# Gather buffers cut from seven to three in an edge-message kernel

## Chip, cores and metric

The kernel runs on one core of one Trainium2 chip. The metric is the device time of one execution in microseconds; lower is better.

## What is computed

A graph layer with N = 6250 nodes of H = 128 features and E = 100000 edges, sorted by target `dst`, each with 4 edge features:

```python
msg_in = jnp.concatenate([node_features[src], node_features[dst], edge_features], axis=1)
h = jax.nn.silu(msg_in @ mW1 + mb1)
messages = h @ mW2 + mb2
aggregated = jax.ops.segment_sum(messages, dst, num_segments=N)
upd_in = jnp.concatenate([node_features, aggregated], axis=1)
u = jax.nn.silu(upd_in @ uW1 + ub1)
updated = u @ uW2 + ub2
return layer_norm(node_features + updated, ln_g, ln_b)
```

The result is added to x and normalized once more. All in float32.

## The kernel before

**Tables.** The product with `mW1` is split by its rows. For all nodes the kernel computes `tab_a = x @ mW1[:128]` and `tab_b = x @ mW1[128:256] + mb1` and stores both in HBM: a loop of 13 blocks for tab_a (L196 to L199), then one for tab_b (L209 product, L211 addition on VectorE into one of three `tb` tiles, L212 store by SyncE's queue). Every edge then needs a row of tab_a by its source, a row of tab_b by its target, and its own 4 features.

**Lists.** Edge features are transposed (L242) and stored (L243), the indices of all groups but the first 14 are loaded (L248, L249), and the targets are made relative to a base node per group (L250). The queue of SyncE in this prologue is in the order written.

**Edges.** Edges go in 98 groups of 1024, eight of 128 each. For a group g:

- `fetch(g)` takes a tile `ga` of 128 x 8 x 128 floats from the pool `gath` and fills it with eight indirect DMAs issued by GpSimd (POOL), one row of tab_a for each edge (L281). In this stage nothing else is on POOL's queue, so POOL runs ahead of the loop as far as free tiles of the pool allow.
- `load(g)` has SyncE load the window of 96 rows of tab_b, the edge features and the targets (L328 to L334); `matrices(g)` makes one-hot matrices of the targets on VectorE (L341, L349).
- `hidden(g)`: TensorE sums the window rows and edge features of each edge (`pre`, L361), VectorE adds the gathered rows (`s = ga + pre`, L363), ScalarE applies silu (L365). The addition L363 is the last reader of `ga`: after it, the tile is free.
- `by_nodes` (L372, L374) sums the messages of one group by node on TensorE, and `add` (L379 to L383) adds the transposed sums into `acc`.

The loop over g issues, in program order, the fetch of a later group, the loads of g+2, the matrices of g+1, `hidden(g)`, `by_nodes(g-1)` and `add(g-2)`. The tile framework puts in the waits, so a gather into a tile waits for the addition L363 of the group that held this tile before.

**Update.** When all groups are summed, the nodes go through the second pair of products and two normalizations (L404 to L499). A second, general path (L502) runs only for lists whose targets don't fit the windows.

Of the kernel before, what the change touches and what calls it, by code (L numbers as in the profile page):

```python
# [24 lines left out]
def kernel(  # L25
# [49 lines left out]
    NW = NP + W  # L75
    K1 = W + ED
    RB = 14
    AHEAD = 4
    LEAD = 2
    FIRST = 14  # L80
    XC = 8
# [101 lines left out]
    with tc.tile_pool(name="tables", bufs=3) as work, tc.tile_pool(  # L183
        name="tables_ps", bufs=2, space=PSUM
# [53 lines left out]
    with tc.tile_pool(name="lists", bufs=1) as work, tc.tile_pool(  # L238
        name="lists_ps", bufs=1, space=PSUM
# [48 lines left out]

    with ExitStack() as edges:
        held = edges.enter_context(tc.tile_pool(name="held", bufs=1))  # L290
        gath = edges.enter_context(tc.tile_pool(name="gath", bufs=AHEAD + 3))
        work = edges.enter_context(tc.tile_pool(name="edge", bufs=3))
        ps = edges.enter_context(tc.tile_pool(name="edge_ps", bufs=2, space=PSUM))

# [11 lines left out]
        def fetch(g):  # L306
            if g >= NG:
                return
            rows[g] = gath.tile([P, G, H], F32, name="ga")
            for i in range(G):  # L310
                gather(rows[g][:, i, :], tab_a, src_i[:, g, i : i + 1])
# [12 lines left out]
        def load(g):  # L324

            if g % RB == 0:
                load_bases(g)
            nc.sync.dma_start(mv[g % NM][:W], tab_b[bass.ds(bases[g], W), :])  # L328
            nc.sync.dma_start(stbuf[g % NST][W:], ea_d[:, g * GE : (g + 1) * GE])
            near[g] = work.tile([W, GE], I32, name="near")  # L330
            n = min(GE, E - g * GE)
            if n < GE:
                nc.vector.memset(near[g][:, n:], N)
            nc.sync.dma_start(  # L334
                near[g][:, :n],
                dst[g * GE : g * GE + n].rearrange("(o e) -> o e", o=1).to_broadcast([W, n]),
            )
# [47 lines left out]
        for g in range(LEAD):  # L385
            load(g)
        for g in range(AHEAD):
            fetch(g)
        oh, h, sw = {0: matrices(0)}, {}, {}
        for g in range(NG + 2):  # L390
            fetch(g + AHEAD)
            if g + LEAD < NG:
# [250 lines left out]
```

## Time and profile before

| | |
|---|---|
| median of 3 runs | 1214.57 us (1214.18 to 1215.01) |
| profiled execution | 1460.16 us, of it the span 1458.3 us |
| mean granted TensorE clock in it | 0.681 |
| busy share of the span: PE, PEld, DVE, ACT, POOL | 56%, 50%, 27%, 14%, 58% |
| gathers (L281) | 784, 1017 ns each |
| DMA | 114.63 MB, mean 79 GB/s |

The profiled execution is 245.6 us longer than the median, far more than the difference between runs, so shares of it can't be carried over to the timed runs without a check. "PE" is TensorE's matmuls, "PEld" its weight loads, DVE VectorE, ACT ScalarE, POOL GpSimd, SP SyncE; a q behind an engine's name means its queue. L281 is line 281. A group's line reads: line, engine, operation, tiles, count, then total busy time, mean ns of one, then the idle time before them and what ended most of it.

### The profile page before, as it was taken

The page shows a single profiled execution, that of the slowest core. Times are in us where ns is not written, and L with a number is a line of the kernel's source. Part 1 is how long each engine was busy: PE and PEld are TensorE (multiplying, and loading weights), DVE is VectorE, ACT ScalarE, POOL GpSimd, SP SyncE. Part 2 cuts the span into 40 slices and gives each one's busy share as a digit, 9 for nine tenths or more (in the row PEclk, how much of TensorE's full clock was granted, in tenths as well). Part 3 has the DMA queues.
Part 4 walks back from the last instruction along what each step waited for, and adds up shares of the span by engine and source line. Part 5 has one row for each costly group of instructions (what it writes and reads, how often), then busy time and mean ns, then how long its engine had stood idle before and what let it go on. Part 6 is the DMA issues. An engine that isn't in the chain of part 4 may idle for free.

```text
span 1458.3 us, 11699 instructions
## 1 busy us (share of the span) xinstructions
PE 816.6 (56%) x3782; PEld 727.7 (50%) x3782; DVE 400.1 (27%) x803; ACT 197.9 (14%) x340; POOL 838.8 (58%) x814
## 2 busy tenths in 40 slices
PE   5410565837564673765726726756576647699700
PEld 5300455727453572655716726745465636594300
DVE  2101331313221231222303303323122212344543
ACT  1002110101110110111101101101011101112254
POOL 3670267657666766766667667666766666604110
PEclk9655566757656775667757757757665666689955
DMA  8424532323232332322323323322322222300011
GB/s 203 121 67 88 103 84 79 100 67 98 83 86 67 87 100 58 95 80 82 91 58 96 89 60 96 89 68 84 87 76 80 82 72 82 90 5 0 2 50 39
DMA packets 100906, 114.63 MB, mean 79 GB/s; under 512 B 42245, under 2 KB 78094, under 8 KB 100758
## 3 DMA queue, kind: packets, MB, share of 16 engines
q1 hardware_dynamic: 72358, 60.68, 14.8%
q0 software_dynamic: 25088, 51.43, 13.8%
q10 hardware_dynamic: 3392, 1.70, 0.5%
q8 instruction: 32, 0.52, 0.1%
q14 instruction: 36, 0.29, 0.1%
HBM read 102.47 MB, written 11.28 MB: 78 GB/s over the span
## 4 chain that ended last, share of the span: by engine, by line
PE 48%; issue 26%; another core or an unknown queue 14%; DVE 4%; ACT 4%; SPq 2%; DMA 1%; POOL 1%; DVEq 0%; ACTq 0%
PE pre L361 23%; PE pw L372 17%; ACT o L490 1%; ACT z L475 1%; SPq L128 1%; PE pa L196 1%; PE ps_y L437 1%; PE ps_a L423 1%; DVE s L363 1%; PE ps_u L427 1%; PE pt L380 1%; DVE st L416 1%; PE ps_u L428 1%; PE ps_a L422 1%
## 5 line engine op out<-in xcount | busy, mean ns | idle before, releaser
L281 POOL DMA_INDIRECT ga<-tab_a,src_i x784 | 797.1, 1017 | 464.9 <-issue 227.4
L361 PE MATMUL pre<-mv,st 100*128 100x128 f32 x1568 | 417.6, 415 | 145.2 <-issue 139.1
L361 PEld LDWEIGHTS pre<-mv,st 100*128 100x128 f32 x1568 | 392.5, 333 | 158.4 <-issue 157.3
L372 PE MATMUL pw<-h,oh 128*96 128x129 f32 x1568 | 301.2, 339 | 271.3 <-issue 266.2
L372 PEld LDWEIGHTS pw<-h,oh 128*96 128x96 f32 x1568 | 258.3, 213 | 310.4 <-issue 305.5
L363 DVE TENSOR_TENSOR s<-ga,pre 128x1024 f32<-128x1024 f32 x98 | 119.3, 1217 | 387.9 <-remote 222.1
L349 DVE TENSOR_TENSOR oh<-w_row,rel 128x768 f32<-128x768 f32 x98 | 93.2, 953 | 409.8 <-remote 322.2
L365 ACT ACTIVATE h<-s 128x1024 f32<-128x1024 f32 x98 | 103.7, 1058 | 629.4 <-DVE s L363 455.0
L374 ACT COPY sw<-pw 96x129 f32<-96x129 f32 x98 | 25.0, 255 | 390.6 <-remote 325.4
L341 DVE TENSOR_SCALAR st<-near,base_p 96x1024 f32<-96x1024 int32 x98 | 75.5, 770 | 4.9 <-DMA near<-in_dst_dram 2.7
L439 POOL TENSOR_TENSOR xu<-x_sb,ub_b 128x512 f32<-128x512 f32 (+1 forms) x13 | 15.6, 1204 | 73.1 <-PE pt L380 41.9
L209 PE MATMUL pa<-w,xT 128*128 128x128 f32 x98 | 19.9, 378 | 63.7 <-issue 38.5
L209 PEld LDWEIGHTS pa<-w,xT 128*128 128x128 f32 x98 | 17.9, 280 | 65.4 <-issue 39.3
L471 POOL TENSOR_TENSOR xb<-x_sb,b_b 128x896 f32<-128x896 f32 x7 | 14.5, 2075 | 48.2 <-DVE z L483 48.2
L383 DVE TENSOR_TENSOR acc<-acc,pt 128x96 f32 x98 | 24.2, 247 | 54.1 <-remote 47.1
L380 PE MATMUL pt<-ident,sw 96*1 96x96 f32 x98 | 26.6, 271 | 14.8 <-issue 14.8
L379 PE MATMUL pt<-ident,sw 96*128 96x96 f32 x98 | 27.3, 279 | 11.8 <-issue 11.6
L211 DVE TENSOR_TENSOR tb<-pa,b 128x512 f32<-128x512 f32 (+1 forms) x13 | 8.5, 660 | 75.8 <-remote 67.3
L379 PEld LDWEIGHTS pt<-ident,sw 96*128 96x128 f32 x98 | 16.6, 169 | 13.8 <-issue 13.3
L383 DVE TENSOR_TENSOR deg<-deg,pt 1x96 f32 x98 | 23.1, 235 | 0.6 <-DVE acc L383 0.6
L242 ACT COPY ea_t<-ea_l 80x5000 f32<-80x5000 f32 x1 | 9.0, 8979 | 85.8 <-DMA mv<-in_L_gnn_mW_dram 85.8
L258 PE MATMUL pf<-ident,far 128*1 128x128 f32 x1 | 0.4, 371 | 36.1 <-DMA b_b<-in_L_gnn_ln_b_dram 36.1
(70 smaller groups left out, 318.3 us busy)
## 6 DMA issues: line engine op xcount, KB each, us to landing
near<-in_dst_dram SPq DMA_DIRECT2D x97, 384.0 KB
ga<-tab_a,src_i POOLq DMA_INDIRECT x784
mv<-tab_b SPq DMA_DIRECT2D x98, 48.0 KB
tab_a<-ta SPq DMA_DIRECT2D x12, 256.0 KB
tab_b<-tb SPq DMA_DIRECT2D x12, 256.0 KB
out_dram<-o SPq DMA_DIRECT2D x6, 448.0 KB
st<-ea_d SPq DMA_DIRECT2D x98, 16.0 KB
ea_l<-in_edge_attr_dram SPq DMA_DIRECT2D x1, 1562.5 KB
```

The source lines that it names most:

```text
L209: nc.tensor.matmul(pb[:, i, :], xT[:, cols], w1[:, 1, :], start=True, stop=True)
L281: nc.gpsimd.indirect_dma_start(out=t, out_offset=None, in_=tab[:, :], in_offset=bass.IndirectOffsetOnAxis(ap=idx, axis=0),)
L341: nc.vector.tensor_scalar(stbuf[g % NST][:W], near.pop(g), base_p[:W, g : g + 1], None, op0=OP.is_equal,)
L349: nc.vector.tensor_tensor(oh, w_row[:, None, :].to_broadcast([P, G, W]), rel[:, g, :, None].to_broadcast([P, G, W]), op=OP.is_equal,)
L361: nc.tensor.matmul(pre[:, i, :], st[:, i, :], mv[g % NM], start=True, stop=True)
L363: nc.vector.tensor_add(s, rows.pop(g), pre)
L365: nc.scalar.activation(h[:, :, :H], s, AF.Silu)
L372: nc.tensor.matmul(pw, oh[:, i, :], h[:, i, :], start=i == 0, stop=i == G - 1)
L374: nc.scalar.copy(sw, pw)
L379: nc.tensor.transpose(pt[:, 0, :], sw[:, :H], ident[:W, :W])
L380: nc.tensor.transpose(pt[0:1, 1, :], sw[:, H:], ident[:W, :W])
L383: nc.vector.tensor_add(at, at, of)
```

## The change

Two numbers change. `AHEAD`, the distance in groups at which `fetch` stands ahead of `hidden` in program order, goes from 4 to 2. The pool of gathered tiles had AHEAD + 3 = 7 buffers; it gets AHEAD + 1 = 3. A gathered tile is 128 x 1024 floats, 512 KB, so 2 MB of SBUF fall free and are not used for anything else. No instruction is added or removed.

```diff
-    AHEAD = 4
+    AHEAD = 2
...
-        gath = edges.enter_context(tc.tile_pool(name="gath", bufs=AHEAD + 3))
+        gath = edges.enter_context(tc.tile_pool(name="gath", bufs=AHEAD + 1))
```

The loop that uses them, unchanged:

```python
for g in range(AHEAD):
    fetch(g)
oh, h, sw = {0: matrices(0)}, {}, {}
for g in range(NG + 2):
    fetch(g + AHEAD)
    if g + LEAD < NG:
        load(g + LEAD)
```

## Prediction

> **What bounds the kernel now.** I read the page's group of gathers first, then the waits of POOL, POOL's timeline, and windows over the stages that these show. Times are microseconds.
>
> The group of L281 and, from the view of the waits of POOL, the lines that belong to it (total, times, longest):
>
> ```profile
> L281 POOL DMA_INDIRECT ga<-tab_a,src_i x784 | 797.1, 1017 | 464.9 <-issue 227.4
> POOL ga L281 <- issue: 227.4, 746, 0.3
> POOL ga L281 <- DVE s L363: 203.9, 25, 57.9
> ```
>
> There are 784 gathers (98 groups of 8), 1017 ns each, with 0.30 between two. "DVE s L363" is the sum that frees a gather buffer: the gather engine stood still for it 25 times. The first time is the longest, and POOL's timeline shows where:
>
> ```profile
> 109.81 0.94 POOL L281 DMA_INDIRECT ga<-tab_a,src_i  x1 [0.30 <-issue]
> 111.06 0.95 POOL L281 DMA_INDIRECT ga<-tab_a,src_i  x1 [0.30 <-issue]
> 169.94 1.21 POOL L281 DMA_INDIRECT ga<-tab_a,src_i  x1 [57.93 <-DVE s L363]
> 171.45 0.94 POOL L281 DMA_INDIRECT ga<-tab_a,src_i  x1 [0.30 <-issue]
> ```
>
> At 112.0 all seven buffers are full (56 gathers since 42.2); the eighth group starts when the first sum has ended, at 169.7. The windows cut there (columns: busy time and count on PE, PEld, DVE, ACT, POOL, then granted clock, DMA share, GB/s):
>
> ```profile
> 42.20:112.10 69.90, 15.05 (x72) 13.79 (x72) 6.13 (x9) 0.00 (x0) 53.01 (x56) 0.56 0.33 86
> 112.10:169.70 57.60, 8.69 (x34) 7.84 (x35) 12.05 (x21) 8.98 (x1) 0.00 (x0) 0.50 0.55 96
> 169.70:1274.40 1104.70, 669.82 (x3106) 618.39 (x3105) 288.14 (x452) 117.84 (x183) 744.11 (x728) 0.67 0.30 82
> 1274.40:1312.00 37.60, 35.36 (x181) 34.66 (x181) 15.98 (x27) 6.53 (x11) 0.00 (x0) 0.80 0.03 7
> 1312.00:1458.30 146.30, 63.58 (x229) 31.06 (x227) 68.23 (x271) 56.01 (x131) 30.02 (x20) 0.74 0.08 23
> ```
>
> The other 24 waits lie in the third window. PE is the cause there. In five-microsecond windows it alternates between a fast pace and one at which an instruction starts only every 0.7 to 2.1:
>
> ```profile
> 870.00:875.00 5.00, 0.75 (x2) 0.23 (x1) 0.96 (x1) 0.26 (x1) 0.00 (x0) 0.50 0.05 13
> 885.00:890.00 5.00, 5.00 (x32) 5.00 (x33) 1.98 (x3) 1.06 (x1) 3.78 (x5) 1.00 0.27 71
> ```
>
> A fast group costs PE 5.8 (pre 3.85, pw 1.77, pt 0.16 in the chain), less than the 10 of eight gathers. A slow stretch of some 25 handles about one group; seven buffers then fill and POOL stops.
>
> **Which of this is in the timed runs?** The profiled execution took 1460.16 (span 1458.3); the runs' median is 1214.57, 245.6 less. I take from the profiled time what a never-waiting POOL would not have: the waits, 203.9; the longer gathers after them (in the timeline the 24 gathers behind a wait sum to 46.8, the other 760 to 750.3, or 0.987 each, so 46.8 - 24 x 0.987 = 23.1); and most of the 37.6 of backlog behind the last gather, since with no backlog only landing and last sum remain, about 10 by my estimate (DMA is quiet 6 after the last gather, the sum is 1.22, the rest margin), which is 27.6. 1460.16 - 203.9 - 23.1 - 27.6 = 1205.6, only 9.0 under the median. So **in the timed runs POOL issues gathers almost from 42.2 to the end**. PE's slow stretches can't be there in that strength, and POOL waits about 9.0 in all. The update behind the edges (146.3) is untouched.
>
> **What the Trainium skill says.** "Perfetto Trace Analysis", Optimization Strategy: the same gap repeated on the engine that should be saturated can mean too few buffers for the next tile. The trace agrees in kind: 24 gaps of 3.0 to 9.0 on POOL, each ended by the sum that frees a buffer. "SBUF — State Buffer", SBUF: two separate sides, says that descriptors of a DMA issued from POOL are made on POOL's cores, and that a DVE operation holding the shared port keeps them from being written. Gathers do vary: 667 of the 760 take 0.94 to 0.96, the other 93 take longer. "TensorE: Matmul & The Clock Gate", Part 1, has the array at half clock after an idle window of about 3.4; the trace grants 0.50 in the slow stretches. At 0.50 a pw of 16 matmuls takes 3.6 instead of 1.94 and pre still 4.0, so a group takes about 8.1, still under 10.
>
> **The change part by part.** POOL's queue holds nothing but gathers in this stage, so issuing `fetch` two groups earlier in program order rather than four moves nothing on it; instructions added or removed: none. No queue is passed. What counts is the pool: group g now reuses the buffer of g-3, not g-7, so the eight gathers of g wait for the sum L363 of g-3. Behind that wait stand only later gathers, and DVE's sums wait for those.
>
> *Start.* POOL fills three buffers by 42.2 + 24 x 1.249 = 72.2 instead of seven by 112.1, then waits for the first sum. Four groups of gathers, 4 x 8 x 1.249 = 40.0, move from beside the table and list stages to behind the first sum, onto the chain that ends last. Their cover was the prologue, and it is gone. When does the first sum end in a timed run? Before: 112.0 + 9.0 = 121.0, if the whole 9.0 is this wait. After: the same or earlier, since fewer gathers run beside the prologue. The trace shows how much they may disturb it (DVE's timeline in the loop that writes tab_b; `[idle <-releaser]` at the end):
>
> ```profile
> 78.96 0.69 DVE L211 TENSOR_TENSOR tb<-pa,b 128x512 f32<-128x512 f32 x1 [16.11 <-remote]
> 101.36 0.69 DVE L211 TENSOR_TENSOR tb<-pa,b 128x512 f32<-128x512 f32 x1 [21.71 <-remote]
> 118.86 0.69 DVE L211 TENSOR_TENSOR tb<-pa,b 128x512 f32<-128x512 f32 x1 [16.81 <-remote]
> ```
>
> While gathers run, an addition waits 16 to 22; after they stop, three follow within 4. An undisturbed floor: the twin loop over tab_a did 13 in 19.9 (19.3 to 39.2), so tab_b would end near 43.3 + 19.9 = 63.2, and from its end (122.9) to the first sum's (169.7) the trace has 46.8: 110.0. I take the middle of 110.0 and 121.0, 115.5. POOL's wait is then 115.5 - 72.2 = 43.3 instead of 9.0: **+34.3**, between +28.8 and +39.8.
>
> *Loop.* With PE at 5.8 to 8.1 a group and POOL at 8 x (0.987 + 0.305) = 10.3, sums follow each group as it lands. The sum of g-3 ends a few microseconds after its own gathers, two groups or 20.6 before POOL wants the buffer. Cost 0; the cover is that 20.6, where it was 62. If sums ever lag by more, POOL is late next, and the first gather behind a wait takes up to 2.1 more often. No view shows an unprofiled lag, so its bounds: none above; below, a gain of at most 33, if all gathers went at 0.944 (784 x 0.043). Value taken 0, because the same DVE operations run beside the same gathers.
>
> Sum: 1214.57 + 34.3 = 1248.9, against the runs' median. The profile's own stretch hardly predicts its successor, for its slow stretches aren't in the runs.
>
> **Rivals.**
> 1. *The prologue gives it all back.* In the profiled execution the first sum ends 57.6 after the last early gather. If that link held in timed runs, it would end at 72.2 + 57.6 = 129.8 instead of 169.7, POOL would resume 39.9 earlier with 40.0 more to do: 1214.7, no change. For it: the delayed additions. Against: before would then hold a 57.9 wait, and 1205.6 + 57.9 = 1263.5 isn't 1214.57, unless each gather is 0.06 shorter in timed runs.
> 2. *Faster: running gathers hold up the others.* PE's slow stretches end when POOL stops (POOL 0.00 in 870 to 875, PE full at 885). If timed gathers all took 0.944, POOL would idle 9.0 + 33 = 42 in all; if such disturbance caused it and the shorter lead removed it all, 42 - 34.3 = 7.7 would be won: 1206.9. It decides only above 34.3 of 42. Against it: nothing less than nearly the whole bound is enough.
> 3. *Three buffers are too few throughout.* If at every second group the sums lag over 20.6, that first gather takes 1.95 instead of 0.987 (46.8 / 24): 48 x 0.96 = 46 more, 1295, and more for the waits themselves. For it: 24 such stops with seven buffers under the profiler. Against it: no room for them in 1214.57.
> 4. *The change isn't what it says:* AHEAD alone would do nothing, but the buffer count is cut too, so this is only a case of 1.
>
> **How the numbers follow.** Forecast 0.80 (own range 1243 to 1255), rival 1 0.06, rival 2 0.06, rival 3 0.08. A difference within 0.2% (2.4) counts as no change; that is about what a measurement here can tell. Slower 0.88, same 0.06, faster 0.06. The range runs from 1222, into cases with part of rival 1, to 1266, with some stops of rival 3.
>
> **What would show it.** In the profile after: the first stretch of gathers is 24, not 56, ends near 72, and the wait for L363 behind it is the longest. In the tab_b loop the additions catch up right after 72 if gathers delay them, and the first sum comes well before 169.7. POOL's waits for L363 after that may be more, from PE's slow stretches alone. Wrong would be a timed result under 1222 or a loop whose gathers take clearly other than 0.99.

## Result and profile after

The median went from 1214.38 us (4 runs) to 1244.88 us (4 runs): ratio 1.0258, 95% interval 1.0240 to 1.0276, slower by 30.5. The forecast was 1248.9, between 1222 and 1266. All times below are microseconds.

In some sets of runs every kernel, the kernel before included, took 1427 to 1451, like the profiled execution that the prediction read (1460): this is called the slow condition below, the other the ordinary one, and a ratio is always to the kernel before in the same set.

The profiled execution of the changed kernel has a span of 1242.5 and took 1244.33, one of its timed runs. The two groups of the page that matter:

```profile
L281 POOL DMA_INDIRECT ga<-tab_a,src_i x784 | 774.1, 987 | 305.5 <-issue 235.6
L363 DVE TENSOR_TENSOR s<-ga,pre 128x1024 f32<-128x1024 f32 x98 | 119.7, 1221 | 689.3 <-DMA ga<-tab_a,src_i 679.3
```

A gather takes 987 ns on the mean, and VectorE's sum waits for gathers to land, not they for it. The view of POOL's waits has one wait for a buffer in the whole execution (total, times, longest):

```profile
POOL ga L281 <- issue: 235.6, 773, 0.3
...
POOL ga L281 <- DVE s L363: 36.6, 1, 36.6
```

POOL's timeline has its place, behind the 24th gather:

```profile
71.55 0.95 POOL L281 DMA_INDIRECT ga<-tab_a,src_i  x1 [0.30 <-issue]
109.11 1.21 POOL L281 DMA_INDIRECT ga<-tab_a,src_i  x1 [36.62 <-DVE s L363]
110.63 0.94 POOL L281 DMA_INDIRECT ga<-tab_a,src_i  x1 [0.30 <-issue]
```

And the windows cut at these points (columns as in the prediction):

```profile
42.60:72.50 29.90, 13.13 (x82) 11.95 (x82) 8.85 (x14) 8.04 (x1) 22.82 (x24) 0.70 0.63 167
72.50:109.10 36.60, 6.05 (x25) 5.79 (x26) 9.56 (x16) 1.13 (x2) 0.00 (x0) 0.50 0.78 122
109.10:1091.80 982.70, 680.35 (x3292) 659.64 (x3291) 294.79 (x480) 127.42 (x195) 751.28 (x760) 0.78 0.35 95
1091.80:1242.50 150.70, 64.14 (x220) 31.89 (x220) 68.92 (x269) 55.85 (x130) 30.02 (x20) 0.72 0.08 22
```

In the second window POOL does nothing; in the third it issues the other 760 gathers without a stop. The end comes 150.7 after the last gather.

### The profile page after: what moved, and what is told of

It reads as the page before. It is cut to its first block, busy times and chain, and to the rows that moved or that the text cites. A ratio compares the mean times of both kernels' runs of the same rounds, so it can differ in the third digit from the quotient of the medians.

```text
span 1242.5 us, 11626 instructions
## 1 busy us (share of the span) xinstructions
PE 788.0 (63%) x3782; PEld 731.5 (59%) x3782; DVE 391.7 (32%) x803; ACT 201.0 (16%) x340; POOL 815.8 (66%) x814
## 4 chain that ended last, share of the span: by engine, by line
POOL 53%; issue 24%; PE 7%; DMA 4%; ACT 4%; DVE 4%; SPq 2%; ACTq 0%; DVEq 0%; POOLq 0%
POOL ga L281 53%; DMA ga<-tab_a,src_i 2%; ACT o L490 2%; ACT z L475 1%; SPq L128 1%; PE pa L196 1%; PE ps_y L437 1%; PE ps_a L423 1%; PE ps_u L427 1%; DVE st L416 1%; PE ps_u L428 1%; PE ps_a L422 1%; DMA tab_b<-tb 1%; ACT ea_t L242 1%; DMA near<-in_dst_dram 1%
## 5 line engine op out<-in xcount | busy, mean ns | idle before, releaser
L281 POOL DMA_INDIRECT ga<-tab_a,src_i x784 | 774.1, 987 | 305.5 <-issue 235.6
L361 PE MATMUL pre<-mv,st 100*128 100x128 f32 x1568 | 415.0, 427 | 249.6 <-issue 244.3
L361 PEld LDWEIGHTS pre<-mv,st 100*128 100x128 f32 x1568 | 387.6, 334 | 265.7 <-issue 265.3
L363 DVE TENSOR_TENSOR s<-ga,pre 128x1024 f32<-128x1024 f32 x98 | 119.7, 1221 | 689.3 <-DMA ga<-tab_a,src_i 679.3
L372 PE MATMUL pw<-h,oh 128*96 128x129 f32 x1568 | 288.3, 360 | 61.8 <-ACT h L365 61.8
L372 PEld LDWEIGHTS pw<-h,oh 128*96 128x96 f32 x1568 | 278.7, 237 | 66.5 <-ACT h L365 66.5
L341 DVE TENSOR_SCALAR st<-near,base_p 96x1024 f32<-96x1024 int32 x98 | 72.1, 736 | 3.8 <-DMA near<-in_dst_dram 3.2
L379 PE MATMUL pt<-ident,sw 96*128 96x96 f32 x98 | 25.7, 262 | 0.8 <-ACT sw L374 0.8
L379 PEld LDWEIGHTS pt<-ident,sw 96*128 96x128 f32 x98 | 24.8, 253 | 1.3 <-ACT sw L374 1.3
L380 PE MATMUL pt<-ident,sw 96*1 96x96 f32 x98 | 25.1, 256 | 0.0
L475 ACT ACTIVATE z<-y,r 128x128 f32<-128x128 f32 x49 | 19.7, 479 | 2.2 <-DVE r L451 2.2
L490 ACT ACTIVATE o<-z,r 128x128 f32<-128x128 f32 x49 | 19.6, 480 | 2.3 <-DVE r L451 2.3
L482 DVE TENSOR_TENSOR z<-z,g_b 128x896 f32<-128x896 f32 x7 | 8.4, 1206 | 32.3 <-ACT z L475 32.3
```

The costliest lines, as they stand in the source:

```text
L281: nc.gpsimd.indirect_dma_start(out=t, out_offset=None, in_=tab[:, :], in_offset=bass.IndirectOffsetOnAxis(ap=idx, axis=0),)
L341: nc.vector.tensor_scalar(stbuf[g % NST][:W], near.pop(g), base_p[:W, g : g + 1], None, op0=OP.is_equal,)
L361: nc.tensor.matmul(pre[:, i, :], st[:, i, :], mv[g % NM], start=True, stop=True)
L363: nc.vector.tensor_add(s, rows.pop(g), pre)
L372: nc.tensor.matmul(pw, oh[:, i, :], h[:, i, :], start=i == 0, stop=i == G - 1)
L379: nc.tensor.transpose(pt[:, 0, :], sw[:, :H], ident[:W, :W])
```

## Experiments

**The kernel before, profiled again** (no edit).

> The kernel before, unchanged, profiled once more. The profile of before that the prediction read took 1460 us against 1214 in the timed runs; the profile of after took 1244 and agrees with its runs. Theory A (that one execution was disturbed, and POOL is never held up for long in an ordinary one): this profile shows a span near 1213, 56 early gathers ending at 112, one short wait of POOL for the first sum of about 6 us, and no stretches in which TensorE starts an instruction only every 0.7 to 2.1 us. Theory B (running seven groups ahead under the profiler makes the slow stretches): a span near 1460 again, with some 24 waits for L363. The timed ratio is 1.000 in both.

Measured: ratio 1.0003 (0.9989 to 1.0017), span 1212.4. Its waits of POOL, the gather behind the 56th, and its windows:

```profile
POOL ga L281 <- DVE s L363: 1.0, 1, 1.0
```

```profile
114.79 1.21 POOL L281 DMA_INDIRECT ga<-tab_a,src_i  x1 [0.98 <-DVE s L363]
```

```profile
42.30:113.80 71.50, 18.68 (x103) 17.37 (x103) 17.45 (x29) 8.99 (x1) 54.66 (x56) 0.61 0.82 161
...
114.80:1059.50 944.70, 734.94 (x3290) 715.02 (x3289) 295.23 (x478) 119.05 (x194) 722.96 (x728) 0.71 0.38 97
1059.50:1212.40 152.90, 66.40 (x222) 33.08 (x222) 69.35 (x271) 56.02 (x131) 30.02 (x20) 0.72 0.08 22
```

In an ordinary execution POOL runs from 42.4 to 1059.4 and waits 1.0 in all, less than the 6 expected. The 24 later stops of the first profile are gone, so theory B is out: seven buffers under the profiler don't make the slow stretches. With this profile the difference adds up from the two traces, before to after:

| term | before | after | difference |
|---|---|---|---|
| first gather starts | 42.4 | 42.7 | +0.3 |
| POOL waits for L363 | 1.0 | 36.6 | +35.6 |
| 784 gathers, summed | 777.6 | 774.1 | -3.5 |
| last gather to end | 153.0 | 150.7 | -2.3 |
| span | 1212.4 | 1242.5 | +30.1 |

**Five buffers.** `AHEAD = 2`, `bufs=AHEAD + 3`.

> AHEAD 2 and five buffers. Theory A: five groups are gathered by 42.7 + 40 x 1.247 = 92.5 us, POOL waits until the first sum's end at 109 to 119, that is 16 to 26 us, so 1208 + 16 to 26 = 1224 to 1234 us, ratio 1.008 to 1.016. Rival (the depth in the loop matters, and five are enough): 1214. Rival (AHEAD in program order is what costs): 1245.

Measured: 1235.65, ratio 1.0168 (1.0136 to 1.0201), 1.7 above the upper end of what was expected. POOL's waits and timeline:

```profile
POOL ga L281 <- DVE s L363: 20.9, 1, 20.9
```

```profile
113.65 1.21 POOL L281 DMA_INDIRECT ga<-tab_a,src_i  x1 [20.92 <-DVE s L363]
```

The wait lies in the expected span: five groups end at 92.7, and the first sum ends at 113.4. Two buffers more than three give back 15.7 of the wait, and 8.6 of the span. The rest are gathers that took 4.7 more in sum than after (778.8), a closing part of 153.7 instead of 150.7, and a start 0.5 earlier. Both rivals, 1214 and 1245 (ratios 1.001 and 1.026), lie outside the interval.

**Seven buffers at the start, three in the loop.** Seven tiles are made by hand, and a group takes one by its number:

```diff
-            rows[g] = gath.tile([P, G, H], F32, name="ga")
+            rows[g] = gtile[held_by(g)]      # g % 7 if g < 21 else 4 + g % 3
```

> The other half: seven buffers for the first 21 groups, then only three of them in rotation. Theory A: 1214 us, ratio 1.00, because by then the lead over the sums has been used up and a sum ends two groups before its buffer is wanted. Rival (three buffers too few in the loop): about 1245, ratio near 1.025, with repeated waits of POOL for L363.

Measured: 1213.8, ratio 1.0008 (0.9986 to 1.0030). Its waits of POOL between 115 and 1065 are these and no others:

```profile
POOL ga L281 <- issue: 218.0, 715, 0.3
POOL ga L281 <- DMA ga<-tab_a,src_i: 3.4, 11, 0.3
POOL ga L281 <- DVE deg L388: 0.6, 2, 0.3
POOL ga L281 <- DVE acc L388: 0.3, 1, 0.3
```

None is for a sum of L363 (L368 in that file), and none is longer than the ordinary 0.3 between two gathers, though from group 21 on only three buffers rotate. In the loop three do what seven do. `AHEAD` is 2 in this kernel, as after, and the time is that of before: the other of the two changed numbers costs nothing.

**Three groups at the start, seven buffers in the loop**, the other half. As above with another `held_by`: group 3 takes the tile of group 0, groups 4 to 7 fresh ones.

> Three groups may be gathered before the first sum, as in the changed kernel, but all seven buffers are used from the fourth group on (group 3 takes the buffer of group 0, groups 4 to 7 fresh ones, the rest rotate over seven). Theory A (the whole loss is the later start of the gathers): 1245 us, the same as the changed kernel, ratio 1.025. Rival (three buffers are too few in the loop): 1214, ratio 1.00.

Measured: 1211.65, ratio 0.9987 (0.9976 to 0.9998); a miss of theory A's number, but the kernel wasn't the one that I meant. In its trace 56 gathers run without a stop before the first sum ends at 112.2, so the framework must have put the gathers into the four fresh tiles ahead of those that wait for tile 0. With GpSimd held to the written order (`tc.manual_schedule`) it was run three times:

> As start3_loop7, but GpSimd's gathers are held to the written order, so the gathers of group 3, which wait for the first sum, can't be overtaken by those of groups 4 to 7 with fresh buffers. Theory A (only the later start costs): three groups end at 72.5, one wait of POOL of about 37 to 41 us follows, time 1243 to 1247, ratio 1.025, though seven buffers are used in the loop. Rival (loop depth): 1214.

> The kernel of start3_loop7_inorder once more, because the four runs of that call, the kernel before among them, were all near 1446 us, as the profile of before that the prediction read. Where the kernel before takes about 1213: theory A (only the later start costs) 1243 to 1247, ratio 1.025, with one wait of POOL of 37 to 41 us after 24 gathers; rival (loop depth) 1213. Where the kernel before takes about 1446: a ratio near 1.00 again, since TensorE's slow stretches set the pace there and not the gathers.

> The kernel of start3_loop7_inorder where the kernel before takes about 1213. Theory A (only the later start costs): three groups end near 72, one wait of POOL of 37 to 42 us follows, 1243 to 1248 us, ratio 1.025, although seven buffers are used in the loop. Rival (loop depth): 1213, ratio 1.00.

All three fell into the slow condition: medians of 1450.9, 1449.52 and 1444.97, against 1446.49, 1445.43 and 1445.29 for the kernel before, each within 0.3% of it. Each shows a stop of 55 to 56 behind the 24th gather, and over 20 more later. This half was therefore not isolated in the ordinary condition. What stands for it is the table above, and five buffers lying between three and seven.

**An earlier first sum.** Three buffers, with the second part of the lists (L248 to L250) moved behind the loads of the first two groups, and the check of the lists (L251 to L261) moved behind the loop:

```diff
         for g in range(LEAD):
             load(g)
+        by_lane(src_i, src, FIRST, NG)
+        by_lane(dst_i, dst, FIRST, NG)
+        relative(FIRST, NG)
```

> The changed kernel (three buffers), with the second part of the index lists loaded only after the loads of the first two groups, and the check of the lists moved behind the loop. Theory A (the loss is the first sum's end less 72.5): the first sum ends near 89 instead of 109, so POOL waits 16 us and the time is 1225, ratio 1.009. Rival (three buffers cost in the loop): 1245.

> The kernel of lists_later_b3 once more. Where the kernel before takes about 1213: theory A (the loss is the first sum's end less 72.5) a first sum near 89, a wait of POOL of 16 us and 1225 us, ratio 1.009; rival (three buffers cost in the loop) 1244, ratio 1.025. Where the kernel before takes about 1446: 0.988 again, as in the first run.

The first run fell into the slow condition: 1427.22, ratio 0.9878 (0.9826 to 0.9931). The second, with the kernel before at 1214.24: 1246.4, ratio 1.0285 (1.0249 to 1.0321). Theory A's 1225 missed, and the number 1244 of the rival came out. The trace says why (POOL's timeline, the windows behind the last gather, and VectorE's timeline there):

```profile
97.36 0.94 POOL L264 DMA_INDIRECT ga<-tab_a,src_i  x1 [25.67 <-DVE s L346]
```

```profile
1086.40:1244.90 158.50, 68.82 (x221) 33.63 (x221) 72.66 (x274) 55.74 (x130) 30.74 (x21) 0.70 0.08 22
```

```profile
1095.55 1.86 DVE L492 TENSOR_TENSOR off<-off 128x784 f32<-128x784 f32 x1
1097.44 0.97 DVE L494 TENSOR_REDUCE far<-off 128x1 f32<-128x784 f32 x1
```

The first sum did move (97.1 instead of 108.8, not to the expected 89), and POOL's one wait fell with it, by 10.9. Two other parts took it back. The moved check now stands on VectorE between the last sum and the update, and the closing part grew by 7.8; that the check is the cause is read from this timeline, not tried apart. And the gathers summed to 780.5, 6.4 more than after, for a reason that no run shows. They began 0.8 earlier: 1242.5 - 10.9 + 7.8 + 6.4 - 0.8 = 1245.0, measured span 1244.9. The rival's mechanism isn't there, since no second wait of POOL for L346 exists. So the run shows the wait following the first sum, not a way to win it.

**Earlier gathers with seven buffers.** `nc.scalar.dma_start(base_i, ...)` in place of `nc.sync.dma_start`.

> The kernel before (seven buffers) with one edit: the load of base_i, which holds VectorE back until 16.3 us ahead of the first transposes' copies, is issued by ScalarE's queue instead of SyncE's. Theory A (from the first gather on, the gathers set the end): tab_a is ready some 4 us earlier, gathers start near 38.5, the time is 1210, ratio 0.997. Rival (something else than the gathers bounds the kernel before): no change, ratio 1.000.

Measured in the slow condition: 1446.57, ratio 1.0000 (0.9978 to 1.0023). The first gather began at 41.3, only 1 earlier than 42.4 and not the expected 4, so it couldn't have told the theories apart.

**Two buffers.** `AHEAD = 1`, `bufs=2`.

> AHEAD 1 and two buffers. Theory A: 16 gathers end at 62.5, POOL waits until the first sum's end near 109, 46.5 us; in the loop the sum of a group ends about 4.5 us after its last gather, still inside the 10.3 us of the next group, so no further waits: 1255 us, ratio 1.033. Rival (waits in the loop once depth is below three): at least 0.96 us for each of some 95 groups, 1340 us or more.

> The kernel of a1b2 where the kernel before takes about 1213. Theory A: 16 gathers end near 62.5, POOL waits until the first sum's end at 109 to 114, 46 to 51 us, and no more in the loop, since a group's sum ends some 4.5 us after its last gather and the next group's gathers take 10.3: 1254 to 1260 us, ratio 1.034 to 1.038. Rival (depth below three makes waits in the loop): 0.96 us or more for each of some 95 groups on top, 1345 us or more.

Both runs fell into the slow condition: 1442.32, ratio 0.9966 (0.9939 to 0.9993), and 1441.47, ratio 0.9998 (0.9970 to 1.0025). Whether two buffers suffice in the loop in the ordinary condition stays open. What they do show is that in the slow one depth is worth nothing: POOL stands still anyway (waits of POOL in the second run),

```profile
POOL ga L281 <- DVE s L363: 222.6, 29, 52.7
```

29 times for 222.6 with two buffers, against 25 times for 203.9 with seven in the profile of the prediction. The first stop hardly depends on the depth there: it is 53 to 55 behind 16 gathers (two buffers), 55 to 56 behind 24, and 58 behind 56. The first sum comes earlier by as much as the gathers stop earlier.

## Why the prediction was right

**The kernel before.** The step that decided was to subtract POOL's waits from the profiled 1460 and to find the timed 1214: "in the timed runs POOL issues gathers almost from 42.2 to the end". The second profile shows just that, with 1.0 of waiting where 9.0 was inferred. Most of the 9.0 is a slip in the subtraction: each of the 25 waits that it took off whole holds the 0.30 that lies between any two gathers, 7.5 in all. Put back, the sum is 1213.1, or 1.5 under the median. (One of the 24 later gaps, given as 3.0 to 9.0, is no more than that 0.30, and the longest gather behind a wait took 2.4, not 2.1.) The traces agree: the ordinary gaps sum to 231.1 in the first profile and to 238.4 in the second. Two smaller errors cancel: 784 gathers took 777.6, not 774.0, and the part behind the last gather 153.0, not 156.4.

**Start.** Predicted: POOL's wait goes from 9.0 to 43.3, +34.3. Measured: from 1.0 to 36.6, +35.6. The term is the time by which the early gathers end sooner less the time by which the first sum does: 39.8 - 5.5 predicted, 41.3 - 5.7 measured. The first part was read from the trace and is sound. That 5.5 and 5.7 agree is luck. The first sum ends at 114.5 before and 108.8 after, where I had 121.0 and 115.5: both about 6.6 too late, which cancels. The 121.0 rested on the 9.0, the 115.5 was the middle between it and the floor of 110.0, and the reason given for the 5.5 isn't the one that the runs show. The two ends, +28.8 and +39.8, hold the measured term.

**What moves the first sum.** Here one step was wrong for the timed runs. I read the additions of the tab_b loop, which waited 16 to 22 in the first profile, as held up by running gathers, and took some of that over. In VectorE's timeline of the changed kernel the loop is through by 60.7, while gathers run until 72.5:

```profile
55.83 0.69 DVE L211 TENSOR_TENSOR tb<-pa,b 128x512 f32<-128x512 f32 x1 [2.15 <-DMA tab_b<-tb]
...
60.43 0.29 DVE L211 TENSOR_TENSOR tb<-pa,b 128x128 f32<-128x128 f32 x1 [0.21 <-DMA tab_b<-tb]
...
94.15 0.86 DVE L223 TENSOR_TENSOR rel<-dst_i,base_b 128x672 f32<-128x672 int32 x1 [17.98 <-DMA dst_i<-in_dst_dram]
```

and in the second profile of before it is as quick with all 56 gathers beside it:

```profile
60.86 0.89 DVE L211 TENSOR_TENSOR tb<-pa,b 128x512 f32<-128x512 f32 x2 [1.01 <-PE pa L209]
...
98.88 0.86 DVE L223 TENSOR_TENSOR rel<-dst_i,base_b 128x672 f32<-128x672 int32 x1 [22.29 <-DMA dst_i<-in_dst_dram]
```

The 5.7 by which the first sum comes earlier after the change arises mostly in the last line: the wait for the second part of the lists is 4.3 shorter where no gathers run beside these loads. SyncE's timeline has the longest step of these loads, first in the changed kernel, then in the second profile of before:

```profile
75.38 10.44 SPq L128 DMA_DIRECT2D src_i<-in_src_dram  x1
```

```profile
75.82 13.25 SPq L128 DMA_DIRECT2D src_i<-in_src_dram  x1
```

In the three other ordinary kernels whose gathers run on beside it (five buffers, and both kernels with seven tiles) it takes 13.0 to 13.2. In the profiles of the slow condition with the lists in their old place it begins after the early gathers have ended and takes 10.4 to 10.5, whether 16, 24 or 56 of them ran. So it is the running gathers that go with the longer loads, whatever the kernel; how they lengthen them, no run shows.

In the slow condition the reading of the tab_b loop holds. With three groups gathered first (the third run in written order) the loop catches up as soon as they end, and the stop is nearly as long as with seven (L369 is the sum L363 in that file):

```profile
71.45 0.94 POOL L281 DMA_INDIRECT ga<-tab_a,src_i  x1 [0.30 <-issue]
127.62 1.20 POOL L281 DMA_INDIRECT ga<-tab_a,src_i  x1 [55.23 <-DVE s L369]
```

```profile
74.95 0.69 DVE L211 TENSOR_TENSOR tb<-pa,b 128x512 f32<-128x512 f32 x1 [13.31 <-remote]
76.42 0.69 DVE L211 TENSOR_TENSOR tb<-pa,b 128x512 f32<-128x512 f32 x1 [0.78 <-remote]
77.81 0.69 DVE L211 TENSOR_TENSOR tb<-pa,b 128x512 f32<-128x512 f32 x1 [0.70 <-PE pa L209]
79.52 0.89 DVE L211 TENSOR_TENSOR tb<-pa,b 128x512 f32<-128x512 f32 x2 [1.01 <-PE pa L209]
```

**Loop.** Predicted cost 0. Right: a single wait after, and a ratio of 1.0008 with three buffers in the loop. In the timeline of after the last sum ends at 1094.8, 3.1 after the last gather's issue, far inside the 20.6 of slack. Gathers took 0.987, as read from the 760 of the first profile that stand behind no later wait.

**What the sum left out.** -3.5 for somewhat shorter gathers, -2.3 behind the last gather and +0.3 before the first. Gathers are long where VectorE works: of those over 1.0, 106 in the second profile of before and 84 after, all but one in each overlap an instruction of VectorE, and none of the 93 and 92 that overlap only the sum L363 is among them. Which instruction does it wasn't tried. That no instruction was added or removed holds for those that count as busy, engine by engine (TensorE 3782, VectorE 803, ScalarE 340, POOL 814 in both); of the others after has 73 fewer. The sentence that no queue is passed holds for POOL only: the framework also put TensorE's instructions in the loop into another order. Around 800 the second profile of before has the products L372, the transposes L379 and L380 and then all of L361; after has ten matmuls of L361 ahead of L372 and six behind it. Whether the 2.3 comes from that wasn't tried. With +35.6 the size comes to +30.1.

**Rivals.** In the ordinary condition the prologue didn't give it back (rival 1): the first sum ends 0.7, 20.7 and 36.3 after the last early gather with seven, five and three buffers. In the slow condition rival 1 is what happens: it ends 52 to 58 after, with 56, 24 or 16 early gathers, and fewer buffers cost nothing. The forecast held because the timed runs were ordinary ones. Rival 3 fell with the loop. Rival 2 fell in the ordinary condition, where POOL had 1.0 to win and not 42, and in the slow one no run shows a clear gain from fewer buffers alone. That the profile of before would hardly resemble the next one was right: their spans are 1458.3 and 1242.5.

## What to carry to other kernels

Prefetch depth can earn twice: in the loop, where it must cover the lag of the consumer, and once at the start, where it lets the bounding engine work while the prologue isn't ready. Here the loop needs three buffers or fewer, and the start uses all seven, at 8 to 10 us of POOL's wait for each (15.7 for the fourth and fifth, 19.9 for the sixth and seventh). By the same sum an eighth would win next to nothing, since only 1.0 of wait is left; that wasn't tried. And before a profile is used, its own time belongs beside the timed runs: what it has too much must be found in its waits, or it can't be trusted. A wait that is taken off so holds the ordinary gap too, which stays.

## What was not expected

Of the five sets of runs behind the experiments, two had the kernel before near 1214 (on chips 7 and 5) and three near 1446 (on chip 2, and twice on chip 15). So it isn't one disturbed execution, as theory A of the second profile had it. No chip showed both conditions, but five sets are too few to call it a matter of the chip. In the profiles of the slow condition POOL's instructions were as quick as ever (mean 0.99 to 1.01 outside the waits), while TensorE had stretches with one instruction per 0.7 to 2.1 (the kernel before) or with none at all for 20 us and more (two buffers, and three groups first). Windows of the second run with two buffers, columns as in the prediction:

```profile
630.00:635.00 5.00, 0.00 (x0) 0.00 (x0) 0.00 (x0) 0.00 (x0) 3.78 (x5) 0.50 0.21 52
640.00:645.00 5.00, 0.64 (x3) 0.61 (x4) 0.98 (x2) 0.95 (x2) 0.00 (x0) 0.50 0.00 1
645.00:650.00 5.00, 5.00 (x24) 5.00 (x24) 2.18 (x4) 0.27 (x1) 1.94 (x3) 0.50 0.34 104
```

The 52 GB/s of the first line is what the gathers alone move by my estimate (128 rows of 512 bytes each 1.249 us), so little else landed then. Many of the stretches ended when POOL stopped, as here, but not all: at 685 in the same profile TensorE is back at 4.94 of 5 while POOL goes on. A further mark separates them: the section of the page on DMA issues gives a time to landing for the gathers in the profiles near 1214 to 1245,

```profile
ga<-tab_a,src_i POOLq DMA_INDIRECT x784, 2.6
```

and none in those of the slow condition, where waits that should name a gather are put down to "remote". What makes the condition stays open.
